# The last block's router logits on VectorE instead of TensorE

## The chip, the core and the metric

The kernel runs on one core of a Trainium2 chip. A core has TensorE (PE in the profile, with its weight loads as PEld), VectorE (DVE), ScalarE (ACT), GpSimd (POOL) and SyncE (SP), each with an instruction queue of its own that is worked off in order; DMA transfers are issued from the queues of SP, ACT and POOL. Operands lie in SBUF (128 partitions), matmul results in PSUM. The metric is the device time of one execution in microseconds, lower is better; the runs shown give a median.

## The reference

One sequence of 2048 tokens of width 512 in float32 passes through a Mamba2 layer with a gated MLP, and then through a mixture of experts. Only the second part is touched:

```python
router_logits = jnp.einsum('bsh,he->bse', x, Wr)      # x: layer-normed tokens, Wr: 512 x 8
probs = jax.nn.softmax(router_logits.astype(jnp.float32), axis=-1)
topk_w, topk_idx = jax.lax.top_k(probs, K)            # K = 2 of E = 8 experts
topk_w = topk_w / jnp.sum(topk_w, axis=-1, keepdims=True)
...
h = jax.nn.silu(g) * u                                # 352 hidden columns per expert
y = jnp.einsum('besi,eih->besh', h, Wd)
out = jnp.einsum('bse,besh->bsh', combine.astype(x.dtype), y)
```

The result is added to the tokens. Each token goes to two experts, so there are 4096 entries of a token and an expert.

## The kernel before

The tokens are 16 row tiles of 128. Mamba runs over them in blocks of 256; the MLP follows in four blocks of 512 tokens (`feed_forward(fb)`, NFB = 4), each over 16 slices of the hidden width. After an MLP block, `route(fb, rows)` normalises its four row tiles, forms their router logits, picks the two best experts of each token, and scatters the entries by indirect DMA into lists in DRAM, one per expert.

`route` for a row tile j: `normed(j)` stores the row to `out` (a DMA on ACT's queue), normalises it into a tile of tag "mid" (L598, VectorE), and stores that to the scratch `xnd`; for the first three blocks also to `xnd1`. `transposed` turns it by four PE transposes (L201) into PSUM and one ACT copy (L203). `logits(j, xT)` is four float32 matmuls of eight columns (L607; two PE instructions each in the trace) and a VectorE copy (L608) into `lg`. After the fourth tile the choice follows (`top` twice, the weights, the running sums), some 25 small VectorE instructions; then two small matmuls `pr` (L654, L655) for the ranks; then positions and eight scatters on POOL (L669).

The experts' work is in tiles of 128 entries of one expert (`tiles()`). For tile s: `gather` fetches the token rows by an indirect DMA on POOL (L1026); `front` transposes them on PE (L201) and copies them on ACT (L203); `hidden` is sixteen PE instructions for gate and up (L1045), then Silu on ACT (L1049) and the product on VectorE (L1050); `turned` transposes the product on PE (L1057) and copies it to SBUF, two thirds on VectorE (L1059) and one third on ACT (L1060); `back` is six PE instructions (L1066), the scaling by the token's weight on VectorE (L1071), and an indirect DMA on POOL that adds the rows to `out` (L1072). All expert weights are in SBUF by then (`load_expert`, during the last MLP block). The order written out is: first half of hidden(s), transposes of turned(s-1), second half of hidden(s), back(s-1).

Which entries a tile has is worked out in tables (`table(n, name, used)`) from the counts per expert and the lists: a matmul of the counts (L936), some VectorE arithmetic, a read of the lists into `rows` by SP (L975) that waits for the scatters, and two matmuls `pi` (L980) that give the tokens and the weights. The first table, of NS1 = 10 tiles, is made from the first three MLP blocks while the last is still running. It holds full tiles only. So the expert tiles can start as soon as the last MLP block is done, with rows from `xnd1`, and the last block's routing and the second table (`NS - NS1` tiles, NS = 39) run alongside them:

```python
work, steps = tiles(), second()
next(feed)
for _ in work:
    next(steps, None)
```

`tiles()` yields once before tile 0, once in tile 0, and twice in each tile after (after hidden(s), and after back(s-1)); at each yield `second()` runs one step: first those of `route` for the last block, then those of the second table. Its first indices are needed by the gather of tile NS1, which is issued two tiles ahead. 36 tiles (NSA) are always run; the rest stand behind a test at the end.

What sets the order: PE's instructions run as written (`manual_schedule`). The other engines' queues are ordered by the planner from its own estimate of the times; of the instructions that are ready it takes the one written first. `tc.issue_after(x)` makes it place an instruction behind x on x's engine. Tiles of one tag share buffers: "mid" has 3, "mg" (MLP weights, 4 KB per partition each) 3, "md" (down weights) 4, and tag "h2T" of the pool `wk` one, which holds the transposed input of the last MLP block until its last product.

Of the kernel before, what the change touches and what calls it, by code (L numbers as in the profile page):

```python
# [9 lines left out]
F32 = mybir.dt.float32  # L10
I32 = mybir.dt.int32
AF = mybir.ActivationFunctionType
ALU = mybir.AluOpType
# [3 lines left out]
P = 128  # L17
T = 2048
D = 512
NK = D // P  # L20
# [8 lines left out]
NFB = T // FB  # L29
# [5 lines left out]
NE = 8  # L35
# [3 lines left out]

NS = (2 * T + NE * (P - 1)) // P  # L40

NS1 = 10


NSA = (2 * T + NE * (P // 2)) // P
# [6 lines left out]


@with_exitstack
def mamba_mlp_moe(ctx, tc, x, w_in, w_out, w_gu, w_down, par, wr, wg, wu, wd, out):

    nc = tc.nc

    def bc(ap, axis, n):
        ap = ap.unsqueeze(axis)
        shape = list(ap.shape)
        shape[axis] = n
        return ap.to_broadcast(shape)
# [7 lines left out]
    pmlp = ctx.enter_context(tc.tile_pool(name="pmlp", bufs=2, side="right"))  # L73
    wk = ctx.enter_context(tc.tile_pool(name="wk", bufs=2, side="right"))
# [21 lines left out]
    def load_w_in(pair):  # L96
# [15 lines left out]
        out=tri, in_=ones, pattern=[[1, P]], compare_op=ALU.is_ge, fill=0.0, base=0, channel_multiplier=-1  # L112
# [3 lines left out]
        out=late, in_=ones, pattern=[[-1, P]], compare_op=ALU.is_gt, fill=0.0, base=0, channel_multiplier=1  # L116
# [16 lines left out]
        out=upto, in_=ones[:, : NE * NE].rearrange("p (e f) -> p e f", e=NE), pattern=[[1, NE], [-1, NE]],  # L133
# [43 lines left out]
    def bank(kind, shape, name):  # L177
        pool, tag = use[kind]
        return pool.tile([P, *shape], F32, name=name, tag=tag)
# [17 lines left out]
    def transposed(src, dst, weight=None, kind="tr"):  # L197

        pt = bank(kind, [NK, P], "pt")
        for k in range(NK):  # L200
            nc.tensor.transpose(pt[:, k, :], src[:, k * P : (k + 1) * P], ident)  # L201
        if weight is None:
            nc.scalar.copy(dst, pt)  # L203
        else:
            nc.vector.tensor_tensor(dst, pt, bc(weight, 2, P), ALU.mult)
# [174 lines left out]
    h2T = [None] * NFB  # L380
# [179 lines left out]
    def mid(shape, name):  # L560
        return wk.tile([P, *shape], F32, name=name, tag="mid", bufs=3)

    NJ = FB // P
    more_rows = None
    mlp_w = None
    newest = None
    NHI = P // NE
    zero = row("zero")
    nc.gpsimd.memset(zero, 0.0)
# [13 lines left out]
    def small(name, *shape):  # L583
        return small_p.tile([P, *shape], F32, name=name, tag=name)

    def route(fb, rows):

        mv2, rs2 = small("mv2", NJ, 2), small("rs2", NJ)
        for j in range(NJ):
            stats(small_p, rows[j], mv2[:, j, :])  # L590
        rsqrt_eps(rs2, mv2[:, :, 1])
        lg, l2, tmp = (small(n, NJ, NE) for n in ("lg", "l2", "tmp"))

        def normed(j):
            t = fb * NJ + j
            nc.scalar.dma_start(out=out[t * P : (t + 1) * P, :], in_=rows[j])
            xn = mid([D], f"xn{t}")
            nc.vector.tensor_scalar(xn, rows[j], mv2[:, j, 0:1], rs2[:, j : j + 1], ALU.subtract, ALU.mult)  # L598
            nc.scalar.dma_start(out=xnd[t * P : (t + 1) * P, :], in_=xn)
            if fb < NFB - 1:  # L600
                nc.scalar.dma_start(out=xnd1[t * P : (t + 1) * P, :], in_=xn)
            return xn

        def logits(j, xT):
            pl = bank("d", [NE], f"pl{fb}_{j}")
            for k in range(NK):
                nc.tensor.matmul(pl, xT[:, k, :], wr_sb[:, k, :], start=(k == 0), stop=(k == NK - 1))  # L607
            nc.vector.tensor_copy(lg[:, j, :], pl)  # L608

        xn = normed(0)  # L610
        yield
        for j in range(NJ):
            if j:
                logits(j - 1, xT)
            xT = mid([NK, P], f"xT{fb}_{j}")
            transposed(xn, xT)
            if j < NJ - 1:
                xn = normed(j + 1)
            yield
        logits(NJ - 1, xT)  # L620

        chosen = [small(n, NJ, NE) for n in ("o1", "o2")]
        m1, m2, *mr = (small(n, NJ) for n in ("rm1", "rm2", "mr1", "mr2"))

        def top(src, mx, mr, oh):

            nc.vector.tensor_reduce(mx, src, AX.X, ALU.max)
            nc.vector.tensor_tensor(tmp, src, bc(mx, 2, NE), ALU.is_equal)
            nc.vector.tensor_tensor(tmp, tmp, bc(rank, 1, NJ), ALU.mult)
            nc.vector.tensor_reduce(mr, tmp, AX.X, ALU.max)  # L630
            nc.vector.tensor_tensor(oh, tmp, bc(mr, 2, NE), ALU.is_equal)

        top(lg, m1, mr[0], chosen[0])
        nc.vector.scalar_tensor_tensor(l2, chosen[0], -3.0e38, lg, ALU.mult, ALU.add)
        top(l2, m2, mr[1], chosen[1])

        wt = [small(n, NJ) for n in ("wt1", "wt2")]
        nc.vector.tensor_tensor(m2, m2, m1, ALU.subtract)
        nc.scalar.activation(m2, m2, AF.Exp)
        nc.vector.tensor_scalar_add(wt[0], m2, 1.0)  # L640
        nc.vector.reciprocal(wt[0], wt[0])
        nc.vector.tensor_tensor(wt[1], m2, wt[0], ALU.mult)


        both, prior = small("both", NJ, NE), small("prior", NJ, NE)
        nc.vector.tensor_tensor(both, *chosen, ALU.add)
        nc.vector.tensor_copy(prior[:, 0, :], before)
        for j in range(1, NJ):
            nc.vector.tensor_tensor(prior[:, j, :], prior[:, j - 1, :], both[:, j - 1, :], ALU.add)
        nc.vector.tensor_tensor(before, prior[:, NJ - 1, :], both[:, NJ - 1, :], ALU.add)  # L650
        yield
        yield
        pr = bank("tr", [NJ, NE], f"pr{fb}")
        nc.tensor.matmul(pr, tri, both, start=True, stop=False)  # L654
        nc.tensor.matmul(pr, ones, prior, start=False, stop=True)  # L655
        nc.vector.tensor_copy(prior, pr)

        for n in range(2):

            at, to = small("at", NJ), small_p.tile([P, NJ], I32, name=f"to{n}", tag=f"to{n}")  # L660
            nc.vector.tensor_tensor(tmp, chosen[n], prior, ALU.mult)
            nc.vector.tensor_reduce(at, tmp, AX.X, ALU.add)
            nc.vector.scalar_tensor_tensor(at, mr[n], -float(T), at, ALU.mult, ALU.add)
            nc.vector.tensor_scalar_add(at, at, NE * T - 1.0)
            nc.vector.tensor_copy(to, at)
            entry = entries[:, n, fb * NJ : (fb + 1) * NJ, :]
            nc.vector.tensor_copy(entry[:, :, 1], wt[n])
            for j in range(NJ):
                nc.gpsimd.indirect_dma_start(  # L669
                    out=writers.pop(), out_offset=bass.IndirectOffsetOnAxis(ap=to[:, j : j + 1], axis=0),  # L670
                    in_=entry[:, j, :], in_offset=None,
                )
            yield
# [117 lines left out]
    for _ in range(3):  # L791
        hT = next(coming)
# [96 lines left out]
    for b in range(NB):  # L889
        fb, at = divmod(b, BPF)  # L890
# [110 lines left out]
    def routed(steps):  # L1001

        nonlocal first
        yield from steps
        first = yield from table(NS1, "1")

# [12 lines left out]
    def of(s):  # L1019

        return (s, first, xnd1) if s < NS1 else (s - NS1, rest, xnd)

# [11 lines left out]
        return xT  # L1034

    def hidden(s, xT):
        n, (exp_i, _, _, _), _ = of(s)
        e = nc.tensor.value_load(exp_i[0:1, n : n + 1], min_val=0, max_val=NE - 1)
        w = ew[:, bass.DynSlice(e, 1), :].rearrange("p a n -> p (a n)")
        pg = bank("g", [EI], f"epg{s}")  # L1040
        pu = bank("u", [EI], f"epu{s}")
        for k in range(NK):
            for a, ps in enumerate((pg, pu)):
                lo = (2 * k + a) * EI
                nc.tensor.matmul(ps, xT[:, k, :], w[:, lo : lo + EI], start=(k == 0), stop=(k == NK - 1))  # L1045
            if k == 1:
                yield
        h = mid([EI], f"eh{s}")
        nc.scalar.activation(h, pg, AF.Silu)  # L1049
        nc.vector.tensor_tensor(h, h, pu, ALU.mult)  # L1050
        return h, w

    def turned(s, h):

        pt = bank("tr", [len(ET), P], f"pht{s}")
        for m, (lo, n) in enumerate(ET):
            nc.tensor.transpose(pt[:n, m, :], h[:, lo : lo + n], ident)  # L1057
        hT = wk.tile([P, len(ET), P], F32, name=f"ehT{s}", tag="a", bufs=4)
        nc.vector.tensor_copy(hT[:, 0:2, :], pt[:, 0:2, :])  # L1059
        nc.scalar.copy(hT[: EI - 2 * P, 2, :], pt[: EI - 2 * P, 2, :])  # L1060
        return hT

# [16 lines left out]
    got, xT = {}, {}  # L1079

    def fetch(upto):

        for s in range(min(upto + AHEAD, NSA if rest else NS1)):
            if s not in got:
# [27 lines left out]
    def second():  # L1112

        nonlocal rest
        yield from feed
        rest = yield from table(NS - NS1, "2", first[-1])

# [6 lines left out]
    with tc.If(filled > NSA - NS1):  # L1124
        for s in range(NSA, NS):
            h, w = finish(hidden(s, front(s, gather(s))))
# [67 lines left out]
```

## Time and profile before

| What | Value |
|---|---|
| median of the runs shown | 1541.85 us (1541.31 to 1543.73, 3 runs) |
| the profiled execution | 1540.27 us |
| its span in the profile | 1538.6 us |
| mean granted TensorE clock | 0.994 |
| PE busy | 1498.3 us, 97% |
| DVE, ACT, POOL busy | 749.8, 744.0, 425.5 us |
| first expert matmul (L1045) | at 1228.90 us |
| indices of the second table (L986) | at 1294.63 us |
| last PE work ends | about 1528 us |

How to read it: the profile is of one execution, by the hardware profiler. A line of a time line has the start, the duration, the engine, the line of the kernel, the operation, the tile written and those read, and in square brackets how long the engine stood idle before it and what ended that. A row of groups has the number of instructions, the busy time and the mean of one. Matmuls overlap one another, so a group of PE instructions lasts a little longer than the distance to the next.

The other lines that matter are shown with the prediction.

### The profile page before, as it was taken

Reading aid. Unit: us, or ns where it says so; the run is one execution under the profiler, and the core shown is the slowest. Engines: PE = TensorE matmul, PEld = TensorE weight load, DVE = VectorE, ACT = ScalarE, POOL = GpSimd, SP = SyncE. Lnnn points to the kernel's source line nnn. Section 1 sums busy time; section 2 is a strip of 40 time slices with the busy share of each in tenths; the row PEclk is TensorE's granted clock in tenths of the full one; section 3 lists DMA queues with packets and bytes.
Section 4 is the critical chain, followed back from the end, with each engine's and each line's share of the span. In section 5 each row is a group of like instructions: output and inputs, shape, how many; then the busy total and the mean of one; then the engine's idle time right before and its main releaser. Section 6 shows DMA issues by size and latency. Waiting matters only on the chain. (4 is left out here: it accounts for less than half of the span.)

```text
span 1538.6 us, 18825 instructions
## 1 busy us (share of the span) xinstructions
PE 1498.3 (97%) x6153; PEld 1021.0 (66%) x6153; DVE 749.8 (49%) x1939; ACT 744.0 (48%) x1332; POOL 425.5 (28%) x537
## 2 busy tenths in 40 slices
PE   8899999999999999999999999999999999999996
PEld 7566577677667676767676677666776666566553
DVE  7776775645645564556454643334343433222221
ACT  5888967635663598458745754222221231111110
POOL 4432324424242212141212120411131124233321
PEclk9999999999999999999999999999999999999999
DMA  9444445545544554454335532426879434333332
GB/s 305 137 138 125 137 140 183 190 149 171 171 151 148 185 165 131 137 118 157 121 123 179 167 121 89 93 93 209 289 205 260 152 91 64 66 69 65 66 63 35
DMA packets 128241, 217.54 MB, mean 141 GB/s; under 512 B 12560, under 2 KB 72848, under 8 KB 128144
## 3 DMA queue, kind: packets, MB, share of 16 engines
q1 hardware_dynamic: 105376, 166.34, 35.6%
q0 software_dynamic: 9088, 18.91, 7.2%
q10 hardware_dynamic: 13680, 31.07, 5.4%
q8 instruction: 52, 0.85, 0.2%
q14 instruction: 45, 0.37, 0.1%
HBM read 175.48 MB, written 40.80 MB: 141 GB/s over the span
## 5 line engine op out<-in xcount | busy, mean ns | idle before, releaser
L691 PE MATMUL pd<-md,a 128*128 128x512 f32 x512 | 238.8, 593 | 0.8 <-DVE r L692 0.7
L340 PE MATMUL pm<-hT,wi 128*128 128x256 f32 x768 | 185.4, 386 | 3.7 <-DMA wi<-in_w_in 3.7
L340 PEld LDWEIGHTS pm<-hT,wi 128*128 128x128 f32 x768 | 141.7, 192 | 29.2 <-issue 7.9
L692 DVE TENSOR_TENSOR r<-r,pd 128x512 f32<-128x512 f32 x128 | 87.4, 684 | 150.6 <-PE pd L691 149.9
L691 PEld LDWEIGHTS pd<-md,a 128*128 128x128 f32 x512 | 96.9, 190 | 76.6 <-issue 65.8
L361 DVE SCALAR_TENSOR_TENSOR ca<-pre,params,ca 128x256 f32<-128x256 f32 x288 | 143.9, 557 | 0.3
L707 PE MATMUL py<-h2T,ms 128*128 128x256 f32 x512 | 131.7, 380 | 3.5 <-DMA ms<-late 2.6
L772 POOL TENSOR_TENSOR a<-a,up 128x256 f32<-128x256 f32 x64 | 47.0, 734 | 265.7 <-DVE up L766 225.8
L340 PE MATMUL pz<-hT,wi 128*128 128x256 f32 x512 | 117.0, 381 | 0.0
L490 PE MATMUL po<-w_o,zs 128*128 128x512 f32 x256 | 116.2, 607 | 0.0
L1045 PE MATMUL epg<-ew,xgT 128*128 x288 | 109.0, 460 | 0.2 <-ACT xgT L203 0.2
L1045 PE MATMUL epu<-ew,xgT 128*128 x288 | 108.7, 459 | 0.0
L707 PEld LDWEIGHTS py<-h2T,ms 128*128 128x128 f32 x512 | 95.4, 190 | 19.5 <-issue 2.3
L420 ACT ACT_TABLE_LOAD x75 | 96.2, 1283 | 21.5 <-DVE ncum L285 14.5
L340 PEld LDWEIGHTS pz<-hT,wi 128*128 128x128 f32 x512 | 94.8, 190 | 13.8 <-ACT zs L373 0.8
L1066 PE MATMUL epd<-ew,ehT 128*128 (+1 forms) x216 | 98.9, 593 | 1.0 <-DVE ehT L1059 1.0
L420 ACT ACTIVATE cum<-cum,ncum 128x128 f32<-128x128 f32 x256 | 85.7, 392 | 6.2 <-POOL cum L314 4.8
L490 PEld LDWEIGHTS po<-w_o,zs 128*128 128x128 f32 x256 | 49.5, 195 | 58.4 <-issue 57.3
L752 ACT COPY a<-px 128x256 f32<-128x256 f32 x64 | 23.6, 369 | 127.2 <-PE px L707 111.3
L1026 POOL DMA_INDIRECT xg<-xnd,idx x36 | 35.5, 985 | 154.4 <-PE pt L201 150.6
L422 DVE SCALAR_TENSOR_TENSOR cum<-cum,dt,psc 128x128 f32<-128x128 f32 x256 | 72.9, 339 | 5.8 <-PE psc L414 3.6
L203 ACT COPY xgT<-pt 128x512 f32<-128x512 f32 x36 | 21.0, 586 | 111.8 <-PE pt L201 111.8
(240 smaller groups left out, 2528.1 us busy)
## 6 DMA issues: line engine op xcount, KB each, us to landing
wi<-in_w_in SPq DMA_DIRECT2D x80, 512.0 KB, 3.8
ms<-late SPq DMA_DIRECT2D x48, 512.0 KB, 3.7
mg<-early SPq DMA_DIRECT2D x48, 384.0 KB, 3.8
md<-in_w_down SPq DMA_DIRECT2D x64, 256.0 KB, 4.0
cum<-rowsd SPq DMA_DIRECT2D x32, 512.0 KB, 4.1
late<-ms ACTq DMA_DIRECT2D x16, 512.0 KB, 2.7
ec<-rowsd SPq DMA_DIRECT2D x60, 128.0 KB, 3.4
xnd<-xn ACTq DMA_DIRECT2D x28, 256.0 KB, 3.8
```

Of the source, the lines that this page charges most:

```text
L340: nc.tensor.matmul(pm[:, m, :], w[:, k, m * P : (m + 1) * P], hT[:, k, :], start=(k == 0), stop=(k == NK - 1))
L361: nc.vector.scalar_tensor_tensor(ca, pre[:, m, k : k + TB], cw[:, k : k + 1], ca, ALU.mult, ALU.add)
L420: nc.scalar.activation(lt[:, half, i], lt[:, half, i], AF.Exp, bias=ncum[:, j, h : h + 1])
L422: nc.vector.scalar_tensor_tensor(lt[:, half, i], lt[:, half, i], dt[:, j, h : h + 1], psc[:, half, i], ALU.mult, ALU.mult)
L490: nc.tensor.matmul(po, y[:, m, :], w_o[:, m, :], start=(m == 0), stop=(m == 7))
L691: nc.tensor.matmul(pd, a[:, j * P : (j + 1) * P], d, start=(m == 0), stop=(m == 1))
L692: nc.vector.tensor_tensor(rows[j], rows[j], pd, ALU.add)
L707: nc.tensor.matmul(ps, w[:, k], m[:, k], start=(first and k == 0), stop=(k == KH - 1), skip_group_check=True)
L772: nc.gpsimd.tensor_tensor(a[:, 1], a[:, 1], up, ALU.mult)
L1026: nc.gpsimd.indirect_dma_start(out=xg, out_offset=None, in_=src, in_offset=bass.IndirectOffsetOnAxis(ap=idx[:, n : n + 1], axis=0))
L1045: nc.tensor.matmul(ps, xT[:, k, :], w[:, lo : lo + EI], start=(k == 0), stop=(k == NK - 1))
L1066: nc.tensor.matmul(pd, hT[:n, m, :], w[:n, NG + m * D : NG + (m + 1) * D], start=(m == 0), stop=(m == len(ET) - 1))
```

## The change

For the last block only, the four normalised row tiles are kept in one tile `kept`, of the tag "h2T". The router's weights come in a second time, transposed to rows (`wr_rows`, 8 x 512), and are read two rows at a time with a broadcast to all 128 partitions into tiles `cols` of tag "mg" (four DMAs of 512 KB on SP's queue). For each expert and row tile one VectorE instruction (`dot`) multiplies the row tile with the row of weights and sums the products along the row into one column of `lg`: 32 of them, in place of sixteen PE transposes, four ACT copies, sixteen matmuls and four VectorE copies. The products themselves go into tiles of tag "md" that nothing reads.

The steps: the four `normed` are done in the first two steps, then two dots a step in sixteen, with the choice behind the last two. Each dot is placed behind `turning`, the newest product L1050 or copy L1059 written so far. The route so takes twelve steps more, which are six tiles, and the first table has 16 tiles instead of 10. The other three blocks route as before.

```diff
-NS1 = 10
+NS1 = 16
...
+        if fb == NFB - 1:
+
+            kept = wk.tile([P, NJ, D], F32, name="kept", tag="h2T", bufs=1)
+
         def normed(j):
             t = fb * NJ + j
             nc.scalar.dma_start(out=out[t * P : (t + 1) * P, :], in_=rows[j])
-            xn = mid([D], f"xn{t}")
+            xn = kept[:, j] if fb == NFB - 1 else mid([D], f"xn{t}")
...
-        xn = normed(0)
-        yield
-        for j in range(NJ):
-            if j:
-                logits(j - 1, xT)
-            xT = mid([NK, P], f"xT{fb}_{j}")
-            transposed(xn, xT)
-            if j < NJ - 1:
-                xn = normed(j + 1)
+        def dot(product, xn, col, j, e):
+            nc.vector.scalar_tensor_tensor(
+                product, xn, 1.0, col, ALU.mult, ALU.mult, accum_out=lg[:, j, e : e + 1]
+            )
+
+        if fb == NFB - 1:
+
+
+            for j in range(NJ):
+                normed(j)
+                if j % 2:
+                    yield
+            for e in range(NE):
+                if e % 2 == 0:
+                    cols = pmlp.tile([P, 2, D], F32, name=f"cols{e}", tag="mg", bufs=3)
+                    nc.sync.dma_start(out=cols, in_=bc(wr_rows[e : e + 2], 0, P))
+                for j in range(NJ):
+
+                    with tc.issue_after(turning):
+                        dot(pmlp.tile([P, D], F32, name="dot", tag="md", bufs=4), kept[:, j], cols[:, e % 2], j, e)
+                    if j == 1 or j == 3 and e < NE - 1:
+                        yield
+        else:
+            xn = normed(0)
             yield
-        logits(NJ - 1, xT)
+            for j in range(NJ):
...
     def hidden(s, xT):
+        nonlocal turning
...
-        nc.vector.tensor_tensor(h, h, pu, ALU.mult)
+        turning = nc.vector.tensor_tensor(h, h, pu, ALU.mult).ins
         return h, w
 
     def turned(s, h):
 
+        nonlocal turning
...
-        nc.vector.tensor_copy(hT[:, 0:2, :], pt[:, 0:2, :])
+        turning = nc.vector.tensor_copy(hT[:, 0:2, :], pt[:, 0:2, :]).ins
...
+        "wr_rows": a["Wr"].T,
```

More of the change, by code (lines that the diff above doesn't have):

```diff
@@ L54, in mamba_mlp_moe @@
 @with_exitstack
-def mamba_mlp_moe(ctx, tc, x, w_in, w_out, w_gu, w_down, par, wr, wg, wu, wd, out):
+def mamba_mlp_moe(ctx, tc, x, w_in, w_out, w_gu, w_down, par, wr, wr_rows, wg, wu, wd, out):
     nc = tc.nc
@@ L566, in mamba_mlp_moe @@
     newest = None
+    turning = None
     NHI = P // NE
@@ L608, in logits @@
             nc.vector.tensor_copy(lg[:, j, :], pl)
-        xn = normed(0)
-        yield
-        for j in range(NJ):
-            if j:
-                logits(j - 1, xT)
-            xT = mid([NK, P], f"xT{fb}_{j}")
-            transposed(xn, xT)
-            if j < NJ - 1:
-                xn = normed(j + 1)
-            yield
-        logits(NJ - 1, xT)
+        def dot(product, xn, col, j, e):
[18 more added lines that the diff above has]
+            xn = normed(0)
+            yield
+            for j in range(NJ):
+                if j:
+                    logits(j - 1, xT)
+                xT = mid([NK, P], f"xT{fb}_{j}")
+                transposed(xn, xT)
+                if j < NJ - 1:
+                    xn = normed(j + 1)
+                yield
+            logits(NJ - 1, xT)
         chosen = [small(n, NJ, NE) for n in ("o1", "o2")]
```

## The prediction

> **What bounds the kernel now.** I read the page's engine totals first, then the stretches behind the last MLP block, then the time line of that stretch instruction by instruction, because the change touches only the last block's routing, which runs between the expert tiles.
>
> ```profile
> PE 1498.3 (97%) x6153; PEld 1021.0 (66%) x6153; DVE 749.8 (49%) x1939; ACT 744.0 (48%) x1332; POOL 425.5 (28%) x537
> ...
> 1228.90:1263.94 35.04, 35.04 (x159) 23.75 (x160) 12.40 (x43) 12.41 (x21) 7.72 (x7) 1.00 0.35 91
> 1263.94:1296.91 32.97, 32.97 (x124) 20.11 (x123) 12.02 (x46) 5.24 (x12) 17.83 (x16) 1.00 0.43 54
> ```
>
> The second and third lines are stretches: span, then busy time of PE, weight load, VectorE (DVE), ScalarE (ACT), GpSimd (POOL), then the granted clock. PE is busy all of both at clock 1.00; VectorE about a third. So work taken from PE here comes off the end, unless VectorE makes PE wait.
>
> How much PE work: the time line gives the start of each expert tile's first matmul (L1045), and what stands between.
>
> ```profile
> 1228.90 0.86 PE L1045 MATMUL epg<-ew,xgT 128*128 x2 [0.24 <-ACT xgT L203]
> 1234.61 0.76 PE L1045 MATMUL epg<-ew,xgT 128*128 x2
> ...
> 1239.68 0.95 PE L607 MATMUL pl<-wr_sb,xT 128*128 128x8 f32 x8
> 1240.49 0.64 PE L201 MATMUL pt<-ident,xn 128*128 128x128 f32 x4
> ...
> 1245.26 0.76 PE L1045 MATMUL epg<-ew,xgT 128*128 x2
> 1255.46 0.76 PE L1045 MATMUL epg<-ew,xgT 128*128 x2
> ```
>
> L607 (logits, eight PE instructions per row tile) and L201 with xn (its four transposes) are what the change takes away.
>
> A tile without routing, and VectorE's dates in it:
>
> ```profile
> 1302.25 0.52 DVE L1050 TENSOR_TENSOR eh<-eh,epu 128x352 f32<-128x352 f32 x1 [1.95 <-PE epu L1045]
> 1304.76 0.75 DVE L1071 TENSOR_SCALAR ey<-epd,tok_w 128x512 f32<-128x512 f32 x1 [1.99 <-DMA out<-ey,idx]
> 1304.99 0.76 PE L1045 MATMUL epg<-ew,xgT 128*128 x2
> 1307.89 0.42 DVE L1059 COPY ehT<-pht 128x256 f32<-128x256 f32 x1 [2.39 <-PE pht L1057]
> 1310.06 2.74 PE L1066 MATMUL epd<-ew,ehT 128*128 x6
> 1313.08 0.76 PE L1045 MATMUL epg<-ew,xgT 128*128 x2
> ```
>
> The period is 1313.08 - 1304.99 = 8.09 us; VectorE has three instructions in it (0.52 + 0.75 + 0.42 = 1.69 us). The copy of ehT ends at 1308.31 and the matmul that reads it starts at 1310.06, its weight load 0.3 us ahead: about 1.4 us to spare.
>
> **Removed from PE.** Tile starts are 1228.90, 1234.61, 1245.26, 1255.46. The first distance, 5.71 us, is of a tile with no down product yet; it holds one set of transposes (0.44 us, from the start of the xn transposes at 1233.74 to that of the next ones at 1234.18). The second, 10.65, is 2.56 over the clean 8.09; the third, 10.20, is 2.11 over. Together 0.44 + 2.56 + 2.11 = 5.11 us. Counted otherwise: 16 transposes and 32 logit instructions at 0.107 us (four in 0.43) are 5.14. I take 5.1 us, all on the path, since PE never stood still there. The four ACT copies (0.58 each) and four VectorE copies (0.17 each) also go; both engines had idle time, so nothing for them.
>
> **Added to VectorE: 32 products with a row sum.** None is in the trace of before. The nearest row is the convolution's, the same operation with both operands in SBUF at half the length.
>
> ```profile
> L361 DVE SCALAR_TENSOR_TENSOR ca<-pre,params,ca x288: 469/475/1491, 16.0 to 918.2; 128x256 f32<-128x256 f32 x144
> ...
> L692 DVE TENSOR_TENSOR r<-r,pd x128: 654/686/690, 254.8 to 1227.8; 128x512 f32<-128x512 f32 x128
> ```
>
> Columns are smallest/median/largest ns. Length costs (684 - 419)/256 = 1.035 ns per column (the means of additions of 512 and 256 columns), so 512 columns are 475 + 265 = 740 ns. The sum must then be written: ACT's operation with a row sum (L504) is followed by a separate read of 186 ns; VectorE's one-column instructions take 155 to 165. Estimate c = 0.74 + 0.17 = 0.9 us. Below: 0.69 with no read and no column scalar. Above: the longest row, 1.491 + 0.265 + 0.186 = 1.94. I take 0.9, being nearest to the median row in operation and operands. 32 x 0.9 = 29 us of VectorE time, over eight tiles, four a tile.
>
> What hides them: each is ordered behind the newest gate product (L1050), or ehT copy, that was issued when it was written down. In program order VectorE then runs, per tile, product, two dots, ey, two dots, ehT copy. First gap: 1302.77 to 1304.76 = 1.99 us for 1.8. Second: 1305.51 to 1307.89 = 2.38 us for 1.8. Nothing is late. If they came in another order, four between ey and the copy would end at 1309.1 and the copy at 1309.5, still ahead of the weight load at 1309.76. VectorE's sum per tile is 1.69 + 3.6 = 5.3 of 8.09. Queued behind each dot is the copy or the product, for which PE waits; behind dots on lacking weights would be everything. PE stalls only when 1302.77 + 4c + 0.75 + 0.42 passes 1309.7, so at c = 1.44: cost zero at 0.9, and up to 8 x (4 x 1.94 - 5.76) = 16 us at the upper bound.
>
> **Weights by DMA.** Four broadcasts of 512 KB on SP's queue. The broadcasts of the same size and form (cum from rowsd, page part 6) land in 4.1 us, 8.5 at most. The buffers of tag mg come free as the MLP ends (last product before 1219), the fourth after the first eight dots. First use is near 1236. They add 2 MB in a stretch where transfers are at 0.43 of their time at most. SP has only the later table's read behind them. Cost 0; if the first were 5 us late, VectorE would hold PE about 3 once.
>
> **Norms and stores moved ahead.** The four normalised tiles (0.55 us each) now follow one another in VectorE from 1231.2 to about 1233.5, into the old place of h2T, free since the MLP. ACT's queue issues four xnd stores (0.33 each) and the out stores earlier; before, the last out store waited behind the first scatter and held ACT 4.19 us with PE still busy. New risk: the first Silu (table load at 1233.39, then 0.46) may be held by up to two such issues, 0.7 us, while PE's need of its product comes 0.44 earlier; spare then was 1236.69 - 1235.70 - 0.44 = 0.55. Cost 0 to 0.2 us; I take 0.1. POOL issues the same gathers and scatters.
>
> **First table of 16 tiles, the route over more tiles.** The route's end moves from the fourth tile to the tenth, the second table from the eighth to the fourteenth, and tiles 10 to 15 take their rows from the first table, which was ready at 1210. Table arithmetic is 16 x 8 and 20 to 23 x 8 columns in place of 10 x 8 and 29 x 8, a few 0.1 us of VectorE with spare time. Steps between the ranks' matmul (pr) and the second table's (pi) are as before; there the rows were issued at 1285.94, landed 3.1 us later, and pi ran at 1293.14, so 4 us to spare. Before pr stands the choice chain, 3.3 us on VectorE, now behind two dots: ready near 1302.77 + 8.2 = 1311.0 in the picture above, pr needed at 1312.2. Cost 0, bound 2 us once.
>
> **Sum.** -5.1 + 0.1 = -5.0 us. The profiled execution took 1540.27 (span 1538.6 and 1.67 around it), so 1535.3; the median, 1541.85, lies 1.58 above it, so I predict **1536.8**, its own range 1535.3 to 1538.5.
>
> **Rivals.** (a) The other side: the dots are slow and VectorE becomes the bound. One mechanism: two SBUF operands contend with POOL. For it:
>
> ```profile
> 108.94 5.15 DVE L361 SCALAR_TENSOR_TENSOR ca<-pre,params,ca 128x256 f32<-128x256 f32 x6
> ...
> 118.73 2.45 DVE L361 SCALAR_TENSOR_TENSOR ca<-pre,params,ca 128x256 f32<-128x256 f32 x6
> ```
>
> The first six ran while POOL did 128x512 sums, and took twice as long. Against: in an expert tile POOL does only two indirect DMA issues, 1.0 + 1.6 of 8.09 us; doubling what runs in those 2.6 us adds at most 2.6 to 5.3. It decides from c = 1.6, where 4c + 1.69 fills the tile and the gain can be gone; at 1.94 VectorE needs 9.45 a tile, 8 x 1.36 = 10.9 us more: 1547.7.
> (b) The dots run at half rate. Then one is 0.21 + 2 x 0.53 + 0.17 = 1.44 us and the margin is just gone: a stall of 0 to 0.5 a tile, 1537 to 1541. Against it: 469 ns for 256 columns is less than half rate alone would need (530). [...]
> (c) The choice chain or the second table is late, and PE waits once, 1 to 3 us: 1538 to 1540. For it: two dots stand before the chain. Against: 1.2 and 4 us to spare.
> (d) The change does nothing to the time, because the seams of the first tiles were as long as the PE work in them: 1541.9. Against: no wait on PE in that stretch.
>
> **How the numbers follow.** Forecast 0.73; (a) 0.08; (b) 0.09; (c) 0.06; (d) 0.04. A measurement of this kernel tells 0.2%, 3.1 us, from no change; so faster is below 1538.8. The forecast, half of (b) less a little and half of (c) lie there: 0.79. Slower: (a), 0.08. Same: 0.13. The range holds the forecast, (c) and most of (b): 1535.0 to 1540.5.
>
> **What would show it.** No L607 and no xn transposes after 1228; tile starts 5.3 and then 8.1 us apart; dots of 0.7 to 0.75 us and a short read behind each; PE busy all through the tiles of the dots. Wrong: idle time ahead of L1066 put down to the ehT copy, dots over 1.4 us, or PE waiting at pr, pi or the transposes of tile 16.

## The result

The changed kernel takes 1539.47 us (median of 19 runs, 1535.31 to 1543.1) against 1545.04 us before (19 runs, 1539.54 to 1550.32). The ratio is 0.9964 with a 95% interval of 0.9954 to 0.9975: 0.36% faster, 5.6 us with an interval of 3.9 to 7.1. The forecast was 5.0 us less, and 1536.8 from a median of before of 1541.85; with more runs that median came out 3.2 us higher, and the changed one with it.

The spans of the two profiled executions differ by 2.0 us only (1538.6 and 1536.6), but they differ before the change begins: the first expert matmul starts at 1228.90 before and at 1231.74 after. From there to the end of the span it is 309.70 us before and **304.86 us after, 4.84 us less**. In the kernels below whose edit does not touch that stretch the distance is the same to a few tenths (with one exception, 305.7), while the start of the first expert matmul varies between 1226.9 and 1240.0 us. Nearly all of that arises before the last MLP block, whose first sums start between 1055.3 and 1066.6 us. So the experiments are judged by two distances, from the first sums of the last MLP block (VectorE) to the first expert matmul, and from there to the end.

### The profile after

The time line of the first tiles of the changed kernel; its columns are start, duration, engine, line, operation, and in brackets the idle time before. (In this kernel L1074 is the expert matmul, L1079 the gate product, L1089 the copy of ehT, L1096 the down matmul, L1101 ey, L616 the dot.)

```profile
1231.74 0.86 PE L1074 MATMUL epg<-ew,xgT 128*128 x2 [0.24 <-issue]
1237.02 0.76 PE L1074 MATMUL epg<-ew,xgT 128*128 x2
...
1242.35 0.52 DVE L1079 TENSOR_TENSOR eh<-eh,epu 128x352 f32<-128x352 f32 x1 [2.01 <-PE epu L1074]
1242.79 0.69 DVE L616 SCALAR_TENSOR_TENSOR dot<-kept,cols 128x512 f32<-128x512 f32 x1
1243.40 0.08 DVE L616 DVE_READ_ACCUMULATOR dot<-kept,cols 128x1 f32 x1
...
1244.63 0.69 DVE L616 SCALAR_TENSOR_TENSOR dot<-kept,cols 128x512 f32<-128x512 f32 x1
...
1245.10 0.76 PE L1074 MATMUL epg<-ew,xgT 128*128 x2
...
1245.24 0.75 DVE L1101 TENSOR_SCALAR ey<-epd,tok_w 128x512 f32<-128x512 f32 x1
...
1248.00 0.42 DVE L1089 COPY ehT<-pht 128x256 f32<-128x256 f32 x1 [2.01 <-PE pht L1087]
...
1250.17 2.74 PE L1096 MATMUL epd<-ew,ehT 128*128 x6
...
1253.18 0.76 PE L1074 MATMUL epg<-ew,xgT 128*128 x2
```

The tiles start 5.28, 8.08 and 8.08 us apart, where before they stood 5.71, 10.65 and 10.20 apart: the transposes of xn and the logit matmuls are gone, and nothing took their place on PE. VectorE works through four dots in one row, 0.61 us from one to the next, between the gate product and ey; ey starts 0.14 us after the next tile's first matmul, where before it started 0.23 us ahead of it (1304.76 and 1304.99), and the copy of ehT is where it was before, 2.9 us behind that matmul. The dots by themselves, smallest, median and largest ns:

```profile
L616 DVE SCALAR_TENSOR_TENSOR dot<-kept,cols x32: 684/686/690, 1242.8 to 1301.2; 128x512 f32<-128x512 f32 x32
L616 DVE DVE_READ_ACCUMULATOR dot<-kept,cols x32: 80/82/84, 1243.4 to 1301.8; 128x1 f32 x32
```

The waits of PE's matmuls for another engine from the first tile on, with total us, times, longest:

```profile
PE epd L1096 <- DVE ehT L1089: 1.0, 2, 0.5
PE pht L1087 <- DVE eh L1079: 0.7, 1, 0.7
```

Both are of the last two tiles, where no next tile covers them; before, they were the same 1.0 and 0.7. No dot made PE wait.

### The profile page after: what moved, and what is told of

It is laid out like the page before. It is cut to its first block, busy times and chain, and to the rows that moved or that the text cites. A ratio compares the mean times of both kernels' runs of the same rounds, so it can differ in the third digit from the quotient of the medians.

```text
span 1536.6 us, 18795 instructions
## 1 busy us (share of the span) xinstructions
PE 1494.7 (97%) x6105; PEld 1016.5 (66%) x6105; DVE 766.3 (50%) x1999; ACT 741.8 (48%) x1328; POOL 425.3 (28%) x537
## 5 line engine op out<-in xcount | busy, mean ns | idle before, releaser
L361 DVE SCALAR_TENSOR_TENSOR ca<-pre,params,ca 128x256 f32<-128x256 f32 x288 | 139.5, 541 | 0.3
L1074 PE MATMUL epg<-ew,xgT 128*128 x288 | 109.0, 460 | 0.2 <-issue 0.2
L1074 PE MATMUL epu<-ew,xgT 128*128 x288 | 108.7, 459 | 0.0
L1096 PE MATMUL epd<-ew,ehT 128*128 (+1 forms) x216 | 99.0, 594 | 1.0 <-DVE ehT L1089 1.0
L1074 PEld LDWEIGHTS epu<-ew,xgT 128*128 128x128 f32 x288 | 54.7, 190 | 30.5
```

Source lines behind the costliest of these rows:

```text
L361: nc.vector.scalar_tensor_tensor(ca, pre[:, m, k : k + TB], cw[:, k : k + 1], ca, ALU.mult, ALU.add)
L1096: nc.tensor.matmul(pd, hT[:n, m, :], w[:n, NG + m * D : NG + (m + 1) * D], start=(m == 0), stop=(m == len(ET) - 1))
```

## The experiments

The two distances in one table, each from one profiled execution, and the ratio to the kernel before with its interval, from several. Kernels whose edit does not touch the last MLP block have 171.0 to 173.3 us there, so a smaller difference than that in the second column says nothing by itself.

| Kernel | last MLP block to first tile, us | first tile to end, us | ratio to before |
|---|---|---|---|
| before | 173.3 | 309.7 | 1 |
| changed | 172.5 | 304.9 | 0.9964 (0.9954 to 0.9975) |
| table of 16 alone | 171.0 | 309.7 | 1.0016 (1.0001 to 1.003) |
| PE work put back | 171.7 | 309.9 | 1.0006 (0.9994 to 1.0018) |
| dots twice | 171.6 | 304.7 | 0.9977 (0.9964 to 0.999) |
| dots three times | 171.6 | 319.1 | 1.0065 (1.0043 to 1.0088) |
| dots unordered | 172.5 | 304.8 | 0.9959 (0.9941 to 0.9978) |
| two blocks | 173.5 | 304.7 | 0.9964 (0.9945 to 0.9982) |
| loads later | 171.2 | 384.9 | 1.0478 (1.0463 to 1.0494) |
| two blocks, late read | 171.4 | 304.8 | 0.9945 (0.9928 to 0.9963) |
| two blocks, late read, loads later | 169.0 | 381.5 | 1.0429 (1.041 to 1.0447) |
| two blocks, spread | 175.6 | 305.7 | 0.9973 (0.996 to 0.9986) |
| changed, again | 172.3 | 305.0 | 0.9962 (0.9947 to 0.9977) |

### Where the gain is from: the table alone, and the PE work put back

The kernel before with one line of the change:

```diff
-NS1 = 10
+NS1 = 16
```

> The kernel before with one part of the change alone: the first table has 16 tiles, the logits stay on TensorE. Measure: the time from the first expert matmul to the end of the span, 309.70 us before and 304.86 after the change. Theory A (the gain is the TensorE work that is gone): no gain, 309.7 within 0.3, ratio to before 1.000. Rival B (the gain comes from the longer first table and the later second one): about 304.9, ratio 0.9965.

Measured: 309.7 us from the first tile to the end; the ratio, 1.0016 (1.0001 to 1.003), is no gain either. The first table of 16 tiles gives nothing by itself; it only makes room for the longer route.

The changed kernel with dead work on PE, once beside each of the dots of experts 0 to 3:

```diff
+        def again(j):
+            pt = bank("d", [NK, P], f"dead{j}")
+            for k in range(NK):
+                nc.tensor.transpose(pt[:, k, :], kept[:, j, k * P : (k + 1) * P], ident)
+            pl = bank("d", [NE], f"dpl{j}")
+            for k in range(NK):
+                nc.tensor.matmul(pl, ident, wr_sb[:, k, :], start=(k == 0), stop=(k == NK - 1))
...
+                    if e < NJ and j == 1:
+                        again(e)
```

> The changed kernel with the TensorE work put back where nothing reads it: four groups of four transposes and four eight-column matmuls beside the first tiles; the dots on VectorE still give the logits. Theory A: 48 instructions at 0.107 us, 5.1 us, all on the path: 310.0 within 0.5 from the first expert matmul to the end, ratio to before 1.000. Rival B: TensorE had time to spare, 304.9, ratio 0.9965.

Measured: 309.9 us, ratio 1.0006. One of the four groups in the trace:

```profile
1238.04 0.60 PE L618 MATMUL dead<-ident,kept 128*128 128x128 f32 x4
1238.47 0.96 PE L621 MATMUL dpl<-wr_sb,ident 128*128 128x8 f32 x8
```

The transposes and small matmuls that nobody reads cost 5.0 us (309.9 - 304.9), which is the whole gain. Theory A holds on both sides, rival B falls: the gain is PE's time, and nothing else of the change is worth more than the few tenths by which this distance varies.

### How much room VectorE has: dots twice, three times, unordered

```diff
-                        dot(pmlp.tile([P, D], F32, name="dot", tag="md", bufs=4), kept[:, j], cols[:, e % 2], j, e)
+                        for _ in range(2):
+                            dot(pmlp.tile([P, D], F32, name="dot", tag="md", bufs=4), kept[:, j], cols[:, e % 2], j, e)
```

> The changed kernel with every dot done twice: eight of 0.61 us in a tile, 4.9 us, under the margin of 5.76 that the prediction worked out. Theory A: no wait on TensorE, 304.9 to 305.4 from the first expert matmul to the end, ratio 0.9965. Rival C (VectorE's lumps already hold TensorE a little, every added dot costs): half of the added 19.6 us or so, 310 to 315, ratio 1.000 to 1.003.

Measured: 304.7 us. Some twenty microseconds more of VectorE work cost nothing, as the margin of 5.76 us a tile says. The trace shows that it was near: the second dot into a column starts 0.73 us after the first, not 0.61, so the eight dots take 5.4 us of a tile, and the copy of ehT behind them ends 0.9 us ahead of the matmul that reads it:

```profile
1251.46 0.42 DVE L1090 COPY ehT<-pht 128x256 f32<-128x256 f32 x1
1252.79 2.74 PE L1097 MATMUL epd<-ew,ehT 128*128 x6
```

(The ratio, 0.9977, is a little above the expected 0.9965, with an interval that holds it; in this profile the first tile began 2.6 us later than in the changed kernel's.) With `range(3)`:

> The changed kernel with every dot done three times: twelve of 0.61 us in a tile, 7.4 us, over the margin of 5.76, and 8.9 us of VectorE with its other three instructions against a period of 8.09. Theory A: TensorE waits for the copy of ehT, 0.8 to 1.5 us in each of eight tiles, 6.8 to 12 us: 311.7 to 317 from the first expert matmul to the end, ratio 1.001 to 1.005. Rival D (the margin is wider, something else takes it up): under 306, ratio 0.9965 to 0.997.

Measured: 319.1 us, 14.2 us more than the changed kernel, and slower than before (1.0065). Theory A's direction is right, rival D falls, but the size is outside what was written down, and the reason shows in the time line of its last tiles with dots:

```profile
1297.51 0.42 DVE L1090 COPY ehT<-pht 128x256 f32<-128x256 f32 x1
1297.98 2.85 PE L1097 MATMUL epd<-ew,ehT 128*128 x6 [1.03 <-DVE ehT L1090]
...
1301.10 0.76 PE L1075 MATMUL epg<-ew,xgT 128*128 x2
...
1311.57 0.74 DVE L1102 TENSOR_SCALAR ey<-epd,tok_w 128x512 f32<-128x512 f32 x1
...
1313.69 0.19 DVE L656 TENSOR_REDUCE rm<-lg 128x4 f32<-128x32 f32 x1
...
1316.49 0.60 PE L683 MATMUL pr<-both,tri 128*128 128x32 f32 x2 [7.58 <-DVE both L675]
...
1318.33 1.38 PE L1075 MATMUL epg<-ew,xgT 128*128 x2
```

The copy of ehT holds PE by 1.03 us here, and by as much or less in three other tiles (these tiles last 8.6 to 9.4 us instead of 8.08, some 4.3 us together). The larger part is one place: the dots end late, the choice (L656 and on) starts at 1313.69, and PE stands 7.58 us at `pr`, the ranks' matmul, which its written order puts before the next tile. And when it goes on, its instructions take nearly twice as long: two expert matmuls 1.38 us instead of 0.76. That leaves some 2.3 of the 14.2 us (14.2 - 4.3 - 7.6). The stretches of that kernel, with the granted clock as the third figure from the end:

```profile
1308.90:1316.50 7.60, 0.01 (x2) 0.04 (x1) 7.08 (x29) 0.20 (x1) 1.77 (x1) 0.65 0.23 31
1317.00:1319.00 2.00, 2.00 (x9) 1.75 (x9) 1.44 (x13) 0.42 (x1) 0.18 (x1) 0.50 0.00 0
1319.00:1321.60 2.60, 2.60 (x6) 1.53 (x5) 0.87 (x5) 0.16 (x1) 1.99 (x3) 0.54 0.31 98
1321.60:1325.00 3.40, 3.40 (x15) 2.26 (x14) 0.42 (x1) 1.70 (x3) 2.71 (x3) 1.00 0.03 3
```

After 7.6 us without work PE was granted about half its clock for nearly 5 us: 0.50 from 1317 to 1319 us, 0.54 from there to 1321.6, and 1.00 again behind that.

Last, the dots without their order:

```diff
-                    with tc.issue_after(turning):
+                    if True:
```

> The changed kernel without the ordering behind the newest product or copy; the planner is free to place each dot as soon as its operands are there. Theory A (VectorE has 5.8 us of room a tile, so the order hardly matters): 304.9 to 305.5 us from the first expert matmul to the end, ratio 0.9965. Rival E (the ordering is what keeps the gain): dots stand in front of products or copies that TensorE waits for, with the first products ahead of the weights: 306 to 310, ratio 0.997 to 1.000.

Measured: 304.8 us, ratio 0.9959. The dots then also run ahead of gate products and copies, six or so at a time, and PE still never waits: with half of VectorE's time free, the order is not what keeps the gain. Rival E falls.

### One block further

If PE's time is all that counts, the third block's logits should be worth the same again. Its routing runs during the last MLP block. The kept rows and all eight rows of weights were put in the space of the last two experts' weights, which come later:

```diff
+        if fb == NFB - 2:
+
+            kept = ew[:, NE - 2, : NJ * D].rearrange("p (j d) -> p j d", j=NJ)
...
+        if fb == NFB - 2:
+            cols = ew[:, NE - 1, : NE * D].rearrange("p (e d) -> p e d", e=NE)
+            nc.sync.dma_start(out=cols, in_=bc(wr_rows, 0, P))
+            for j in range(NJ):
+                normed(j)
+            yield
+            for e in range(NE):
+                for j in range(NJ):
+                    with tc.issue_after(turning):
+                        dot(mid([D], "dot"), kept[:, j], cols[:, e], j, e)
+                if e < NE - 1:
+                    yield
...
-        if n % 4 == 2:
+        if n % 4 == 2 or n % 4 == 0 and 4 <= n < 36:
```

> The change carried one block further: the third block's logits too by VectorE, four dots in each half slice of the last MLP block, behind the newest product there; its kept rows and all eight rows of weights lie in the space of the last two experts until these are loaded. Theory A: another 5.1 us of TensorE work gone, ratio to before 0.993; a further saving of 3 to 5 us in the last MLP block. Rival F: in that block VectorE has five instructions a slice that TensorE waits for within 0.4 to 1 us, and dots of 0.61 us in front of them take the gain back: ratio 0.996 to 0.999.

Measured: ratio 0.9964, the last MLP block 173.5 us: nothing gained beyond the change. PE's work did go, and as much came back as idle. That stretch of the changed kernel and of this one; behind the limits stand its length and PE's busy time:

```profile
1059.20:1231.80 172.60, 168.90 (x663) 117.92 (x661) 72.57 (x188) 39.46 (x92) 29.46 (x61) 1.00 0.80 245
1061.50:1235.10 173.60, 164.84 (x615) 112.41 (x614) 92.07 (x248) 37.30 (x88) 33.42 (x61) 1.00 0.81 256
```

Rival F named the wrong place, though: PE waits 5.5 us in all for late weights (`ms`), where in the changed kernel it was 1.7, and the largest single wait leads not to VectorE but to SP. The waits of SP's queue, and what followed:

```profile
SPq L1018 <- DMA lists<-entries,to: 9.3, 3, 6.8
```

```profile
1147.58 0.33 SPq L1018 DMA_DIRECT2D rows<-lists  x1
...
1148.47 0.45 SPq L547 DMA_DIRECT2D ms<-late  x1
```

```profile
1154.72 1.10 PE L750 MATMUL py<-h2T,ms 128*128 128x256 f32 x4 [2.75 <-DMA ms<-late]
```

The steps behind the dots had been brought closer together, so the table's read of the lists stood in SP's queue while the scatters were still landing, up to 6.8 us at a time, and the weights of the next MLP slice were queued behind it; PE then waited 2.75 us for them. Not all of the late weights are from there: a wait of 1.81 us that ends at 1142.26 is for a load that SP had issued at 1130.77, ahead of the read, and that took over 11 us to land. So the read was put back to the old distance (`n < 20` in place of 36). To tell this (theory G) from a stage that is limited by its transfers (rival H; 44 MB go in 174 us, the queues' share is 0.81), another kernel moved 11 of the 24 parts of the expert weights behind the first tiles, alone and together with the two blocks:

```diff
-        if n % 5 in (0, 2) and parts:
+        if n % 5 == 0 and parts:
...
+        newest = h
...
     for _ in work:
         next(steps, None)
+        if parts:
+            load_expert(*parts.pop(0))
```

> The changed kernel with the expert weights spread differently: 13 of 24 parts in the last MLP block, the other 11 during the first expert tiles. Measure: the last MLP stage, from its first sums on VectorE to the first expert matmul, 172.5 us in the changed kernel, 171.0 to 173.3 in the runs whose edit does not touch it, and 173.5 in the run with two blocks by dots, where 5.1 us less were hoped for. Theory G (in the run with two blocks, SP's queue stood at the read of the lists and held the weight loads behind it): the transfers themselves are no limit, 169 to 172, ratio 0.995 to 0.997. Rival H (the transfers limit this stage): with 7 of 42 MB gone 165 to 168, ratio 0.992 to 0.994. From the first expert matmul to the end: 304.9 to 306.

> The run with two blocks by dots again, with the steps behind the dots at their old distance, so that the read of the lists stands 19 us or more behind their scatters instead of 10. Theory G: SP waits under 1 us at the read, the 4.6 us that TensorE waited for late weights there go, last MLP stage 167 to 169.5 us, ratio 0.993 to 0.995. Rival H: the gain stays lost to transfers, 171 to 174, ratio 0.996 to 0.997.

> Two blocks by dots with the late read, and the later expert loads. Theory G: about the sum of the two, last MLP stage 166 to 169 us, 304.9 to 306 from the first expert matmul to the end, ratio 0.992 to 0.994. Rival H: 160 to 164, ratio under 0.991. Rival I (the moved loads hold up the gathers of the first tiles): over 307 from the first expert matmul to the end.

Measured, for the loads: with 7 of 42 MB gone the last MLP block takes 171.2 us, inside the range of the kernels whose edit does not touch it. Rival H's large gain did not come, but this run could not have shown it: in the changed kernel PE is busy 168.85 of the 172.5 us here, so no more than 3.7 us were to be had. What did go is PE's wait for late weights, 1.7 us there and none here. As a kernel it is worthless, since from the first tile to the end it takes 384.9 us instead of 304.9. Neither theory had that, and rival I named another cause:

```profile
PE epd L1097 <- DMA ew<-in_wg: 11.4, 2, 5.7
PE epd L1097 <- DMA ew<-in_wd: 11.3, 2, 5.8
PE epg L1074 <- DMA ew<-in_wd: 11.2, 2, 6.5
```

The first tiles now wait for loads that are just on their way, ten times in all, 3.9 to 6.5 us each and 53 us together. Much of the rest of the 80 us is the expert matmuls themselves: by the pages they were busy 342.2 us here (115.5 + 114.8 + 111.9) and 316.7 in the changed kernel (109.0 + 108.7 + 99.0), and the longest single one of L1074 into epg took 0.93 us instead of 0.56. The granted clock, at 9 tenths or more on both sides of it, stands at 7, 7 and 8 tenths in the page's three slices from 1255 to 1376 us. Of which expert a tile is, is known only on the chip, and its matmuls read the weights' tile at a place from a register; that they therefore wait for every load into that tile, whichever expert it is for, was argued from the code and not tested.

Measured, for the late read: SP's wait at the lists is gone (0.9 us, for another load), the last MLP block takes 171.4 us instead of 173.5, ratio 0.9945. By PE's waits that is better than with the early read (late weights 3.3 us instead of 5.5); by time it is not shown, since the intervals of the ratios overlap and 2.1 us is within what this block varies by. It is short of theory G's 167 to 169.5. PE is busy 164.79 of 171.4 us and idle for the rest, 3.3 us of it for late weights and 1.6 for a copy on ACT (in two waits). With the later loads as well it was 169.0, 2.2 less than the later loads alone, with late weights at 1.6: of the 4 us taken from PE, about 2 reach the end of that block in these two profiles. So transfers do hold back a part of the second block's gain, as rival H had it, though not the amount that it named.

A last version took out what the trace still showed, the four stores at once on ACT's queue and the one large transfer of weights:

```diff
             for j in range(NJ):
                 normed(j)
-            yield
+                yield
             for e in range(NE):
+                if e % 2 == 0:
+                    nc.sync.dma_start(out=cols[:, e : e + 2], in_=bc(wr_rows[e : e + 2], 0, P))
```

> Two blocks by dots, with what was still in its way taken out: one row tile is normalised and stored per step instead of four at once, the weights come in four transfers instead of one, and the table's read of the lists is at its old step. Theory G: ACT's wait behind the four stores (1.4 us on TensorE) and the burst of transfers at the start go, last MLP stage 167 to 170 us against 172.5 of the changed kernel, ratio 0.993 to 0.995, below the changed kernel's beside it. Rival H: transfers are near their limit in this stage and the rest of the gain is lost there, 171 to 173, ratio as the changed kernel's.

> The changed kernel on the same chip as the run beside it, for a direct comparison: ratio to before 0.9955 to 0.9975, last MLP stage 171 to 173, 304.9 us from the first expert matmul to the end.

Measured: 175.6 us for the last MLP block, ratio 0.9973 (0.996 to 0.9986), beside 172.3 us and 0.9962 (0.9947 to 0.9977) for the changed kernel on the same chip. Both theories missed. The time line and the stretches there:

```profile
1086.15 0.33 ACTq L607 DMA_DIRECT2D xnd<-ew  x1
1086.51 0.37 ACT L796 COPY a<-px 128x256 f32<-128x256 f32 x1 [4.60 <-DMA ms<-late]
...
1086.94 2.07 PE L751 MATMUL px<-ts,mg 128*128 128x256 f32 x4 [3.34 <-ACT a L796]
```

```profile
1083.60:1086.90 3.30, 0.00 (x0) 0.00 (x0) 0.00 (x0) 0.39 (x2) 0.00 (x0) 0.81 1.05 410
1086.90:1091.00 4.10, 4.06 (x10) 3.25 (x11) 0.17 (x1) 0.63 (x2) 0.00 (x0) 0.50 1.06 411
```

ACT's copy stands in its queue behind a store of a normalised row, while the DMA engines are full (1.05; what that store itself waited for is open); PE waits 3.34 us for it and then has half its clock for the next 4 us, so its four matmuls take 2.07 us instead of 1.03. The four norms still came close together, now at the start of that block's traffic. So the changed kernel was not clearly beaten: the best of the three, 0.9945, has an interval (0.9928 to 0.9963) that overlaps the changed kernel's (0.9954 to 0.9975), and the others do not lie below it. Whether another place for the third block's norms and stores would bring the rest out is open.

## Why the prediction was right

**What bounds it.** Right: PE's work in the first tiles was all on the path. Put back as dead work, it costs the 5.0 us again.

**The PE work removed.** 5.1 us less 0.1 forecast, 4.84 measured from the first expert matmul to the end. At the tile starts that it was read from it is all there: the first three distances add up to 26.56 us before and 21.44 after, 5.12 less; where the 0.3 goes on the way to the end was not followed. The 0.1 for a held Silu did not show: it starts 5.79 us after the first expert matmul in both kernels.

**The price of a dot.** 0.9 us was too much: 0.686 for the product and 0.082 for the read, 0.61 from start to start, so 19.6 us of VectorE time and not 29. The length was scaled from the convolution's row, which takes 475 ns where 128x256 additions take 419; that its column scalar is the reason was not tested. An addition of 512 columns, 686 ns, was the right row. ACT's 186 ns did not carry over to VectorE's read, 82 ns. It made no difference to the sum, being hidden either way; the kernels with two and three times the dots show where it would.

**The margin.** The dots ran four in a row between the product and ey, an order of which the prediction gave no dates (it had two and two, and four between ey and the copy); its sum for the margin, which has the four dots and ey ahead of the copy, covers it. 1.44 us a dot as the point where PE waits fits: with two dots for one, 1.34 us, nothing; with three, about 2.0, waits in half the tiles. The one-off at the choice chain, bounded at 2 us, was the wrong bound for slow dots: the lag of VectorE gathers there, and with three times the dots it was 7.6 us and the clock. In the changed kernel too the room was largely used up in the tile where the choice falls: the copy of ehT started 1.1 us late (1305.71), which is most of the 1.4 us it had to spare.

**The rivals.** (a) Contention with POOL did not show, but in the changed kernel it had no occasion to: none of the 32 dots ran while POOL issued an indirect DMA. In the kernel with dots three times, ten ran wholly or in part beside the three issues between 1293.8 and 1305.0 us (1.78, 0.98 and 1.77 us long), and each took 0.68 or 0.69 us, as without: those issues did not lengthen a dot. The row that the rival rested on, the six convolutions of 5.15 us, ran beside elementwise work on POOL. (b) Half rate did not show either, in no run: the 512 columns of a product took 686 ns, where that rival had 0.21 + 2 x 0.53 us, and 686 is the time of an addition of that length (686 with one operand in PSUM, 688 for `ts` with both in SBUF). (c) pr, pi and the transposes of tile 16 waited for nothing. (d) fell with the dead work, which cost 5.0 us where it was put.

**What else had been set at nothing.** The weights' transfers, the norms moved ahead and the longer table did cost nothing: the first two tiles start 5.28 us apart, as the removal alone gives, and the table of 16 alone leaves 309.7 us.

## What to carry to other kernels

Where one engine is busy all through a stage, work moved from it comes off the end nearly in full (4.84 of 5.1 us here), and the other engine's time counts only from the point where the sum of one period, or the lump in front of an instruction that the first engine waits for, passes the room there (no wait at 1.34 us for the dots of a column and row tile, waits in half of the tiles at about 2.0); work out that point, since far below it the price may be wrong by half. A step that is cheap in one stage can be lost in the next, if its loads and stores stand in a queue in front of others' work (SP stood up to 6.8 us at the read of the lists with weights behind it, and PE then waited 2.75). And the waits of 3.34 and 7.58 us on TensorE that are shown here cost more than themselves: the granted clock was 0.50 in the stretches of 4.1 and 2.0 us behind them.

## What the runs showed that was not expected

The row sum of a dot showed as a read of 82 ns behind a product of 512 columns that took 686 ns, as an addition of that length does, and the instructions overlap: 0.61 us from one dot to the next, less than the 0.686 of the product alone (0.73 where both write the same column). In the 4.1 us after a wait of 3.34 us on PE the granted clock was 0.50. The time of this kernel varied by several microseconds in a part that no edit to the expert tiles touched: the first sums of the last MLP block came between 1055.3 and 1066.6 us, and in two profiles of the changed kernel itself at 1059.2 and 1064.6; what causes this is open.
